# Other places for the sorted tokens, and other steps for the pairs, at the end of attention with routed experts on one core

## The chip, the core and the metric

The kernel runs on one core of a Trainium2 chip. A core has five engines that run beside each other, each with a queue of its own: TensorE (PE; its weight loads are PEld), VectorE (DVE), ScalarE (ACT), GpSimd (POOL) and SyncE (SP, which here issues most of the transfers). The metric is the device time of one execution in microseconds. A profile is a record of one execution; its span runs from the first to the last instruction of the program.

## What is computed

Four sequences of 1024 tokens with 512 features pass through attention with 16 heads of 32, then through a layer of 8 experts of rank 64 of which each token takes one; each half has a residual and a layer norm without weights.

```python
# x: (4, 1024, 512); wq, wk, wv, wo: (512, 512); A: (8, 64, 512); B: (8, 512, 64)
scores = einsum('bqhd,bkhd->bhqk', xq, xk)          # no scaling
probs  = softmax(scores)
x = layernorm(x + einsum('bhqk,bkhd->bqhd', probs, xv) @ wo.T)
p = softmax(x_flat @ Wr.T + br)
expert_idx, expert_weight = argmax(p), max(p)
h = einsum('nd,erd->ner', x_flat, A)
y = einsum('ner,eor->neo', h, B) / 64
x = layernorm(x + y[expert_idx] * expert_weight)
```

Everything is float32.

## The kernel before

**Attention.** A unit is one sequence and a group of four heads (GH = 4), 16 units in all; the last four, from LAST = 12 on, belong to the last sequence. Queries go in chunks of QC = 256 (NQ = 4 chunks), keys in tiles of 128 (NK = 8). `scores(s)` multiplies queries with keys (L290) and VectorE takes row maxima (L292); after every eighth step GpSimd splits the maxima into three bf16 parts (L192 to L197), which `turn_m` turns (L303). `weigh(s)` puts the maxima into four PSUM banks (L321), adds keys times queries (L330), and ScalarE takes exponentials into `probs` (L340). The sums of the exponentials, `dens`, are added by GpSimd (L344, L352) as long as maxima are still being taken 16 steps ahead, and by VectorE after that. `combine` multiplies with the values (L369) at every fourth step, and `settle` sums `dens` over keys (L388), takes the reciprocal on VectorE (L391) and scales (L393).

**After attention.** Class `After` treats one sequence. `project` multiplies with wo (L449) and adds the residual, `norm`, `choose` and `gate` make the first layer norm and the choice of the expert. `count` and `assign` give each token a place in a list sorted by experts, `scatter` (L561, an indirect DMA from GpSimd) writes tokens to `sorted_x` in device memory. Then the sorted tokens are treated in pairs of tiles of 128: `load_tokens` (L578, SyncE) reads pair k back, `turn_tokens` turns it (L607), `up` multiplies with A (L614), `down` with B (L623), VectorE adds (L626), `weigh_y` takes statistics (VectorE L409 to L411, GpSimd L402 to L404), `norm_y` scales (L414), and `store` writes two tiles to `out` with indirect DMAs from GpSimd (L641). The first three sequences have 8 pairs, the last has 7: its last 256 queries go through class `Last`, which multiplies with all experts at once (L726), masks (L734, L736), multiplies back (L741), adds (L745), and stores without sorting (L755).

**Tiles in rings.** A tile with a tag takes a place of a ring. Tag "h" has NT = 8 places of 128 x 514 and holds tokens of the sequences before sorting and, as `x`, after it; the last sequence's unsorted tokens lie elsewhere. So the two tiles of pair k take the places of pair k - 4, also across the border between two sequences, and their load waits for that pair's stores. Tag "k" has 5 places, one for the keys of each unit. Tag "probs" has 4.

**The order.** A loop runs over steps; step i weighs weights[i - 16] and takes scores of maxima[i], so that N = 272 is the first step after the last weighing. All else is a list of pieces. A `Piece` has a cost, a first and a last step, pieces that it comes after by a gap of steps, and things to be done so many steps later (`then`). A planner fills the steps in turn: it takes a piece that is due, or, while a step's cost is below a level worked out from what is left, one that is allowed. `r.step(k)` is the piece of a sequence's pairs: it holds `up` of pair k - 1, `down` of pair k - 2 and `turn_tokens` of pair k. Its `then` puts the statistics of pair k - 2 one step later, the norm GAP and the stores GAP + 1 steps later. `load_tokens(k)` stands one step ahead of piece k, the weights at pieces k and k + 1. At the end `keep_order` fixes this order on each engine, SyncE's too[...].

The steps of `r.step(k)` that the planner gives are, for the third sequence, 229, 234, 237, 240, 244, 250, 254, 261, 264, 268, and for the last, 265, 266, 269, 270, 272, 274, 275, 276, 278. The queries left to `Last` are projected in step 273, `up` is in 277, `mask` in 278, `down` in 279. The lines that set this are

```python
TAIL = [(N - 7, N - 6), (N - 6, N - 4), (N - 4, N - 3), (N - 3, N - 2)]
TAIL += [(N + i, N + i) for i in (0, 2, 3, 4, 6)]
...
            if b < B - 1:
                first, last_ = end + 17 + 3 * k, end + 25 + 4 * k
            else:
                first, last_ = TAIL[k]
```

where `end` is the step behind a sequence's last unit, 208 for the third.

Of the kernel before, what the change touches and what calls it, by code (L numbers as in the profile page):

```python
# [9 lines left out]
F32 = mybir.dt.float32  # L10
# [4 lines left out]
ALU = mybir.AluOpType  # L15
# [3 lines left out]
P = 128  # L19
HD = 32  # L20
GH = P // HD
QC = 256
# [19 lines left out]
def attention_then_experts(  # L42
# [18 lines left out]
    pe, act, dve, pool, sync = nc.tensor, nc.scalar, nc.vector, nc.gpsimd, nc.sync  # L61
    B, S, D = x.shape
    E = wr.shape[1]
    C = D // P
    NK = S // P
    NQ = S // QC
    TQ = QC // P
    NS = 2 * NK
    KP = NK // 2
# [4 lines left out]
    NT = S // P  # L74
    NX = 2 * NT
    W = D + 2
# [5 lines left out]
    work = ctx.enter_context(tc.tile_pool(name="work", bufs=2))  # L82
# [7 lines left out]
    def bank():  # L90
        turn_of[0] += 1
        return banks[(turn_of[0] - 1) % len(banks)]
# [32 lines left out]
    power = const.tile([P, TQ], F32, tag="power", name="power")  # L125
# [3 lines left out]
    for e in range(E):  # L129
# [5 lines left out]
        out=before_f,  # L135
# [33 lines left out]
    for t in spread_m:  # L169
# [5 lines left out]
        out=expand_f,  # L175
# [7 lines left out]
    expand = const.tile([E, E * R], BF16, tag="expand", name="expand")  # L183
# [25 lines left out]
    qT, kT, vS, mT, aT, top, probs, dens, both = ({} for _ in range(9))  # L209
# [51 lines left out]
    def project_k(u, x):  # L261

        if x.n == 0:
            kT[u] = work.tile([P, S], F32, tag="k", name="k", bufs=5)
        ps = bank()[:, :QC]
        for c in range(C):
            pe.matmul(ps, wk_sb[:, c, ts(units[u][1], P)], x.x[:, c, :], start=(c == 0), stop=(c == C - 1))  # L267
        act.copy(kT[u][:, ts(x.n, QC)], ps)
# [128 lines left out]

    def finish_stats(mv):

        rs = work.tile([P, 2, TQ], F32, tag="rs", name="rs", bufs=4)  # L400
        var = work.tile([P, TQ], F32, tag="var", name="var")
        pool.tensor_scalar_add(var, mv[:, :, 1], EPS)  # L402
        pool.tensor_tensor(rs[:, 0], var, power, ALU.pow)
        pool.tensor_tensor(rs[:, 1], mv[:, :, 0], rs[:, 0], ALU.mult)  # L404
        return rs

# [6 lines left out]
    def apply(h, rs, i):  # L413
        act.activation(h, h, AF.Identity, bias=rs[:, 1, i : i + 1], scale=rs[:, 0, i : i + 1])  # L414
# [42 lines left out]
    def stored(i):  # L457

        for other in stores:
            tc.declare_no_dep(i, other, reason="other rows")  # L460
        stores.append(i)

    class After:
# [110 lines left out]
        def load_tokens(self, k):  # L574
            assert len(self.scatters) == self.nt
            for i in range(2):
                self.x[k, i] = work.tile([P, W], F32, tag="h", name="x", bufs=NT)
                load = sync.dma_start(self.x[k, i], sorted_x[self.b][ts(2 * k + i, P), :]).ins  # L578
                for other in self.scatters:
                    tc.add_manual_dep(  # L580
                        load,
                        other.name,
                        mybir.DependencyInfo(mybir.DependencyClass.Sync, mybir.DependencyReason.DATA),
                        reason="any row",
                    )
# [81 lines left out]
    class Last:  # L667
# [58 lines left out]
                pe.matmul(ps, places["wu"][:, c, ts(k, P)], self.hT[:, c, :], start=(c == 0), stop=(c == C - 1))  # L726
            act.copy(self.u[:, k, :], ps)

        def mask(self):

            for k in range(0, C, 2):
                ps = bank()
                for i in range(2):
                    pe.matmul(ps[:, ts(i, QC)], expand[:, ts(k + i, P)], self.oT, start=True, stop=True)  # L734
                u = self.u[:, k : k + 2, :]
                dve.tensor_mul(u, ps.rearrange("p (i q) -> p i q", q=QC), u)  # L736

        def down(self, i, half):
            ps = bank()[:, :H2]
            for k in range(C):  # L740
                pe.matmul(  # L741
                    ps, self.u[:, k, ts(i, P)], places["wd"][:, k, ts(half, H2)], start=(k == 0), stop=(k == C - 1)
                )
            h = self.h[i][:, ts(half, H2)]
            dve.scalar_tensor_tensor(h, ps, self.gate[:, i : i + 1], h, ALU.mult, ALU.add)  # L745
            if half == 0:
                return
            if i == 0:
                self.mv = work.tile([P, TQ, 2], F32, tag="y_mv", name="y_mv2")
            self.add(self.mv, i)  # L750

        def finish(self):
            self.norm()
            for i in range(TQ):
                stored(sync.dma_start(out[B - 1, ts(TQ * self.n + i, P), :], self.h[i]).ins)  # L755

    N = len(weights) + NS
    COST_S, COST_T, COST_AV = 4 * 512, 512 + 4 * 512, 4 * NK * QC  # L760
    HALF = 4 * C * QC
# [27 lines left out]
    for i in range(len(weights)):  # L789
        base[i] += COST_S  # L790
        base[i + NS] += COST_T
        u, c, kp = weights[i]
# [18 lines left out]
    for u in range(1, LAST):  # L811
        for n in range(NQ):
            x_in = Load(units[u][0], n)
            first = max(start_of(u - 3) + KP * (n + 1), 0)
            for f in (project_q, project_k):
                Piece(lambda f=f, u=u, x_in=x_in: f(u, x_in), HALF, first, start_of(u - 1) - 1, load=x_in)
    for gs in ((0, 1), (2,), (3,)):
        for n in range(NQ):
            x_in = Load(B - 1, n)
            for g in gs:  # L820
                u = LAST + g
                first = max(start_of(LAST - 3) + KP * (g + 1), start_of(LAST - 4 + g))
# [3 lines left out]
    for n in range(1, NQ):  # L826
        for pair in ((0, 1), (2, 3)):
            x_in = Load(B - 1, n)
            first = start_of(LAST - 3 + n) + KP * (pair[1] + 1)
# [20 lines left out]
        return lambda i: i + k + (i + k in busy)  # L850


    TAIL = [(N - 7, N - 6), (N - 6, N - 4), (N - 4, N - 3), (N - 3, N - 2)]
    TAIL += [(N + i, N + i) for i in (0, 2, 3, 4, 6)]
    GAP = [2] * (B - 1) + [1]
    for b, r in enumerate(rest):
        end = start_of(C * b + C)
        for i in range(4):
            part = sorted_x[b].rearrange("(i j p) w -> i p j w", p=P, i=4)[i]
            early[min(start_of(b * C + i), start_of(LAST)) + 6 + (b == B - 1) * i].append(  # L860
                lambda part=part: sync.dma_start(part, nothing.unsqueeze(1).to_broadcast((P, NX // 4, W)))
            )
        p = None
        for t in range(r.nt):
            n, i = divmod(t, TQ)
            first = end - NS + KP * (n + 2)
            last_ = first + 5
            if b == B - 1:
                first = start_of(LAST) + NS * (n + 1) + KP
                last_ = first + 5  # L870
                if n == NQ - 2:
                    first = last_ = start_of(LAST) + NS * (n + 1) + 1 + i
            for half in range(2):
                then = []
                if i == TQ - 1 and half == 1:
                    if b < B - 1 or n < NQ - 2:
                        then = [(2, 0, r.norm, n), (step_without(2), 0, r.choose, n), (step_without(4), 0, r.gate, n)]
                    else:
                        then = [(1, 0, r.norm, n), (1, 0, r.choose, n), (2, 0, r.gate, n)]
                    if b < B - 1 and n == NQ - 1:  # L880
                        then += [(step_without(3), 600, r.count), (step_without(4), 0, r.assign)]
                        then += [(5 + k // 2, 0, r.scatter, k) for k in range(NT)]
                    elif b == B - 1 and n == NQ - 2:
                        then += [(2, 600, r.count), (3, 0, r.assign)]
                        then += [(3 + k // 3, 0, r.scatter, k) for k in range(r.nt)]
                p = Piece(
                    lambda r=r, t=t, half=half: r.project(t, half),
                    HALF,
                    first,
                    last_,  # L890
                    after=[(p, 0)] if p else (),
                    load=loads.setdefault((b, n), lambda r=r, n=n: r.load(n)),
                    then=then,
                )
        for k in range(r.nx // 2 + 2):
            if b < B - 1:
                first, last_ = end + 17 + 3 * k, end + 25 + 4 * k
            else:
                first, last_ = TAIL[k]
            p = Piece(  # L900
                lambda r=r, k=k: r.step(k),
                3 * 2200,
                first,
                last_,
                after=[(p, 3 if b < B - 1 else 1) if k else (p, 11 if b < B - 1 else 6)],
                then=[(-1, 0, r.weigh_y, k - 2), (GAP[b], 0, r.norm_y, k - 2), (GAP[b] + 1, 0, r.store, k - 2)]
                if k >= 2
                else [],
            )
            r.steps.append(p)  # L910
    last = {}

    def on_last(n, f, *args):
        def run():
            if n not in last:
                last[n] = Last(n)
            getattr(last[n], f)(*args)

        return run
# [15 lines left out]
                then=then,  # L935
            )
    for k in range(C):
        ups.append(Piece(on_last(n, "up", k), HALF, N + 5, N + 5, after=[(p, 4)]))
    q = Piece(on_last(n, "mask"), 1024, N + 6, N + 6, after=[(o, 1) for o in ups])
    for i in range(TQ):  # L940
        for half in range(2):
            done = i == TQ - 1 and half == 1
            then = [(1, 0, on_last(n, "finish"))] if done else []
            Piece(on_last(n, "down", i, half), HALF, N + 7, N + 7, after=[(q, 1)], then=then)

# [141 lines left out]
```

## Time and profile before

| | us |
|---|---|
| three runs | 1526.82, 1527.3, 1531.33 (median 1527.3) |
| the profiled execution | 1522.7 |
| its span | 1520.9 |
| TensorE busy | 1451.4 (95%) |
| GpSimd busy | 1186.0 (78%) |
| VectorE busy | 992.9 (65%) |
| ScalarE busy | 749.7 (49%) |
| GpSimd's additions L352 and L344 | 837.7 and 141.4 |
| TensorE's mean granted clock | 0.983 of full speed |

Busy shares are means over stages with different limits[...]. So the page is read for where the digits of a row change along the span, and then stretch by stretch: busy time of each engine in a stretch, what each engine waited for, and the chain of waits, which follows the last instruction back to what released it. In a row of the timeline stand start, duration, engine (with a q for its queue), line, operation, tiles written and read, shapes, count, and in brackets the engine's idle time before it and what ended that.

### The profile page before, as it was taken

To read this page: it belongs to the slowest core of one execution; us is meant where nothing else is said; L and a number is where in the kernel's file an instruction comes from. 1 tells how busy PE (TensorE), PEld (TensorE's weight loads), DVE (VectorE), ACT (ScalarE), POOL (GpSimd) and SP (SyncE) were. 2 spreads that over 40 slices of the span, in tenths; PEclk is the share of its full clock that TensorE was granted. 3 is DMA by queue.
4 is the path that set the end of the run, shared out by engine and by line. 5 is a ranking of instruction groups with operands and counts; after the bars stand their busy time and mean duration, and the time that the engine had idled before them with its cause. 6 is when DMAs were issued, how large, how long until landed. Compare 5 with 4: busy or idle time off the path is not lost.

```text
span 1520.9 us, 37286 instructions
## 1 busy us (share of the span) xinstructions
PE 1451.4 (95%) x15100; PEld 933.0 (61%) x15100; DVE 992.9 (65%) x1853; ACT 749.7 (49%) x1527; POOL 1186.0 (78%) x949
## 2 busy tenths in 40 slices
PE   7999999999999999999999999999999999999675
PEld 6666666666666666666666666666666565555344
DVE  1546666666776576676677557776877668776743
ACT  1125555554445555555444546555445556565532
POOL 2019999998778899899878988999998999972333
PEclk9999999999999999999999999999999999999877
DMA  7422212122102524332110523433411402221241
GB/s 236 139 83 72 71 43 71 43 85 84 57 16 84 167 82 142 107 104 71 33 52 30 181 65 118 153 99 103 139 67 57 149 19 67 81 66 57 77 146 42
DMA packets 101051, 135.25 MB, mean 89 GB/s; under 512 B 9077, under 2 KB 71301, under 8 KB 100880
## 3 DMA queue, kind: packets, MB, share of 16 engines
q1 hardware_dynamic: 91072, 113.92, 23.8%
q0 software_dynamic: 7696, 16.85, 3.1%
q8 instruction: 119, 1.95, 0.5%
q10 hardware_dynamic: 2112, 2.10, 0.4%
q14 instruction: 52, 0.43, 0.1%
HBM read 99.70 MB, written 41.52 MB: 93 GB/s over the span
## 4 chain that ended last, share of the span: by engine, by line
PE 79%; POOL 7%; ACT 4%; DVE 4%; issue 3%; DMA 2%; POOLq 0%; SPq 0%; ACTq 0%; DVEq 0%
PE bank L369 13%; PE bank L290 12%; PE bank L330 12%; PE bank L276 8%; PE bank L257 8%; PE bank L267 7%; PE bank L449 7%; POOL dens L352 5%; PE bank L321 5%; ACT probs L340 3%; PE bank L388 2%; PE bank L623 2%; PE bank L607 1%; PE bank L614 1%; DVE top L292 1%
## 5 line engine op out<-in xcount | busy, mean ns | idle before, releaser
L352 POOL TENSOR_TENSOR dens<-dens,probs 128x1024 f32<-128x1024 f32 x355 | 837.7, 2360 | 92.7 <-ACT probs L340 71.8
L292 DVE TENSOR_REDUCE top<-bank 128x1 f32<-128x512 f32 x1024 | 635.9, 683 | 416.2 <-PE bank L290 416.0
L340 ACT ACTIVATE probs<-bank 128x512 f32<-128x512 f32 x1024 | 528.3, 602 | 278.1 <-PE bank L330 262.0
L290 PE MATMUL bank<-k,q 32*128 32x512 f32 x2048 | 287.1, 594 | 1.2 <-DVE slot_i L541 0.8
L330 PE MATMUL bank<-q,k 32*128 32x256 f32 x4096 | 268.6, 376 | 0.0
L369 PE MATMUL bank<-probs,v 128*32 128x256 f32 x4096 | 237.0, 381 | 1.8 <-ACT probs L340 1.7
L330 PEld LDWEIGHTS bank<-q,k 32*128 32x128 f32 x4096 | 202.7, 185 | 18.3 <-issue 2.6
L369 PEld LDWEIGHTS bank<-probs,v 128*32 128x32 f32 x4096 | 129.4, 110 | 100.2 <-ACT probs L340 20.4
L344 POOL TENSOR_TENSOR dens<-probs 128x1024 f32<-128x1024 f32 x60 | 141.4, 2356 | 8.8 <-ACT probs L340 8.5
L257 PE MATMUL bank<-xT,wq 128*128 128x256 f32 x512 | 128.5, 395 | 8.7 <-DMA xT<-in_xt 7.9
L449 PE MATMUL bank<-wo,aT 128*128 128x264 f32 (+1 forms) x512 | 122.2, 389 | 6.0 <-ACT probs L340 4.3
L257 PEld LDWEIGHTS bank<-xT,wq 128*128 128x128 f32 x512 | 93.6, 192 | 55.9 <-ACT probs L340 33.2
L290 PEld LDWEIGHTS bank<-k,q 32*128 32x128 f32 x2048 | 110.9, 184 | 26.5 <-issue 5.4
L267 PE MATMUL bank<-xT,wk 128*128 128x256 f32 x512 | 123.7, 386 | 3.2 <-ACT probs L340 3.1
L276 PE MATMUL bank<-wv,xT 128*128 128x256 f32 (+1 forms) x512 | 124.3, 390 | 1.2 <-ACT probs L340 0.7
L391 DVE RECIPROCAL bank<-bank 128x256 f32<-128x256 f32 x64 | 112.5, 1758 | 18.6 <-PE bank L388 18.6
L449 PEld LDWEIGHTS bank<-wo,aT 128*128 128x128 f32 x512 | 94.4, 190 | 41.6 <-ACT probs L340 26.6
L267 PEld LDWEIGHTS bank<-xT,wk 128*128 128x128 f32 x512 | 94.9, 190 | 38.3 <-ACT probs L340 26.3
L276 PEld LDWEIGHTS bank<-wv,xT 128*128 128x128 f32 x512 | 93.9, 190 | 34.6 <-ACT probs L340 17.5
L321 PE MATMUL bank<-mT,ones_b 3*128 3x512 bf16 x1024 | 108.5, 387 | 3.6 <-ACT probs L340 1.7
L377 ACT COPY both<-bank 128x256 f32<-128x256 f32 x64 | 23.8, 373 | 176.7 <-PE bank L369 176.7
L641 POOL DMA_INDIRECT out<-x x62 | 63.3, 1021 | 33.0 <-issue 15.3
(132 smaller groups left out, 974.0 us busy)
## 6 DMA issues: line engine op xcount, KB each, us to landing
xT<-in_xt SPq DMA_DIRECT2D x98, 512.0 KB, 3.6
sorted<-nothing SPq DMA_DIRECT2D x16, 1028.0 KB, 7.0
x<-sorted SPq DMA_DIRECT2D x62, 257.0 KB, 3.0
wa<-in_wa SPq DMA_DIRECT2D x62, 128.0 KB, 2.2
wb<-in_wb SPq DMA_DIRECT2D x62, 128.0 KB, 3.2
h<-in_x SPq DMA_DIRECT2D x28, 256.0 KB, 3.8
wo<-in_wo POOLq DMA_DIRECT2D x1, 1024.0 KB, 6.2
wv<-in_wv ACTq DMA_DIRECT2D x2, 512.0 KB, 13.1
```

The source lines that it names most:

```text
L257: pe.matmul(ps, wq_sb[:, c, ts(units[u][1], P)], x.x[:, c, :], start=(c == 0), stop=(c == C - 1))
L267: pe.matmul(ps, wk_sb[:, c, ts(units[u][1], P)], x.x[:, c, :], start=(c == 0), stop=(c == C - 1))
L276: pe.matmul(ps, x.x[:, c, ts(t, P)], wv_sb[:, c, columns(h)], start=(c == 0), stop=(c == C - 1))
L290: pe.matmul(ps, q[r, ts(t % TQ, P)], kT[u][r, ts(n, 512)], start=True, stop=True)
L292: dve.tensor_reduce(top[i][:, here // 2, j, n : n + 1], ps, axis=AX.X, op=ALU.max, negate=True)
L321: pe.matmul(ps.rearrange("p (k q) -> p k q", q=QC), ones_b[r, :], m[r, :].unsqueeze(1).to_broadcast((NP, 2, QC)), start=True, stop=False,)
L330: pe.matmul(ps[:, ts(k, QC)], kT[u][r, ts(2 * kp + k, P)], qT[u, c][r, :], start=False, stop=(k == 1),)
L340: act.activation(pr[:, :, j, :], ps.rearrange("p (k q) -> p k q", q=QC), AF.Exp)
L344: adder.tensor_add(dens[u, c], pr[:, 0].rearrange("p j q -> p (j q)"), pr[:, 1].rearrange("p j q -> p (j q)"),)
L352: adder.tensor_add(dens[u, c], dens[u, c], pr[:, k].rearrange("p j q -> p (j q)"))
L369: pe.matmul(ps[j * HD : (j + 1) * HD, :], v[:, k, col : col + HD], probs[u, c, k // 2][:, k % 2, j, :], start=(k == 0), stop=(k == NK - 1),)
L449: pe.matmul(ps, aT[b, c, n][:, ts(i, P)], wo_sb[:, c, columns(half)], start=(c == 0), stop=(c == C - 1))
```

## The change

The sorted tokens of the last sequence's pairs 0 to 4 lie in the ring "k", one place for both tiles of a pair, and the places of this ring become 128 x 1028 instead of 128 x 1024. Pairs 5 and 6 stay in "h".

```diff
-            kT[u] = work.tile([P, S], F32, tag="k", name="k", bufs=5)
+            kT[u] = work.tile([P, max(S, TQ * W)], F32, tag="k", name="k", bufs=5)
...
-                self.x[k, i] = work.tile([P, W], F32, tag="h", name="x", bufs=NT)
+                if self.b < B - 1 or k >= 5:
+                    self.x[k, i] = work.tile([P, W], F32, tag="h", name="x", bufs=NT)
+                elif i == 0:
+
+                    pair = work.tile([P, max(S, TQ * W)], F32, tag="k", name="x_pair", bufs=5)
+                    self.x[k, 0], self.x[k, 1] = (pair[:, ts(j, W)] for j in range(TQ))
```

The third sequence's pieces get steps of their own (SPREAD, counted from step 208), and the last sequence's get later ones (TAIL). The pieces of `project` of the first three sequences are bound to two steps.

```diff
-    TAIL = [(N - 7, N - 6), (N - 6, N - 4), (N - 4, N - 3), (N - 3, N - 2)]
-    TAIL += [(N + i, N + i) for i in (0, 2, 3, 4, 6)]
+    SPREAD = [18, 21, 24, 28, 30, 33, 36, 40, 42, 45]
+    TAIL = [(N - 4, N - 4), (N - 3, N - 3), (N - 2, N - 2)] + [(N + i, N + i) for i in (0, 2, 3, 4, 5, 7)]
...
-            first = end - NS + KP * (n + 2)
-            last_ = first + 5
+            first = end - NS + KP * (n + 2) + 1
+            last_ = first + 1
...
-            if b < B - 1:
+            if b < B - 2:
                 first, last_ = end + 17 + 3 * k, end + 25 + 4 * k
+            elif b == B - 2:
+                first = last_ = end + SPREAD[k]
             else:
                 first, last_ = TAIL[k]
...
-                after=[(p, 3 if b < B - 1 else 1) if k else (p, 11 if b < B - 1 else 6)],
+                after=[(p, 3 if b < B - 2 else 1) if k else (p, 11 if b < B - 1 else 9)],
```

The planner then gives 226, 229, 232, 236, 238, 241, 244, 248, 250, 253 for the third sequence and 268, 269, 270, 272, 274, 275, 276, 277, 279 for the last.

In `Last`, `up` and `mask` go by halves (two blocks of `up` in step 277 and two in 278, the masks one step behind each), `down` is in step 280, and each row of tokens has statistics by halves, a norm and a store of its own; `finish` is gone, and `finish_stats` takes one column or two.

```diff
     for k in range(C):
-        ups.append(Piece(on_last(n, "up", k), HALF, N + 5, N + 5, after=[(p, 4)]))
-    q = Piece(on_last(n, "mask"), 1024, N + 6, N + 6, after=[(o, 1) for o in ups])
+        ups.append(Piece(on_last(n, "up", k), HALF, N + 5 + k // 2, N + 5 + k // 2, after=[(p, 4)]))
+        if k % 2:
+            q = Piece(on_last(n, "mask", k - 1), 512, N + 6 + k // 2, N + 6 + k // 2, after=[(ups[-1], 1)])
...
             if half == 0:
+                self.st = work.tile([P, 2, 6], F32, tag="st2", name="st2")
+            dve.bn_stats(self.st[:, half, :], h)
+            if half == 0:
                 return
-            if i == 0:
-                self.mv = work.tile([P, TQ, 2], F32, tag="y_mv", name="y_mv2")
-            self.add(self.mv, i)
-
-        def finish(self):
-            self.norm()
-            for i in range(TQ):
-                stored(sync.dma_start(out[B - 1, ts(TQ * self.n + i, P), :], self.h[i]).ins)
+            mv = work.tile([P, 1, 2], F32, tag="y_mv2", name="y_mv2")
+            dve.bn_aggr(mv[:, 0, :], self.st)
+            dve.tensor_scalar_mul(mv[:, 0, 0:1], mv[:, 0, 0:1], -1.0)
+            apply(self.h[i], finish_stats(mv), 0)
+            stored(sync.dma_start(out[B - 1, ts(TQ * self.n + i, P), :], self.h[i]).ins)
```

More of the change, by code (lines that the diff above doesn't have):

```diff
@@ L398, in finish_stats @@
     def finish_stats(mv):
-        rs = work.tile([P, 2, TQ], F32, tag="rs", name="rs", bufs=4)
-        var = work.tile([P, TQ], F32, tag="var", name="var")
+        n = mv.shape[1]
+        rs = work.tile([P, 2, TQ], F32, tag="rs", name="rs", bufs=4)[:, :, :n]
+        var = work.tile([P, TQ], F32, tag="var", name="var")[:, :n]
         pool.tensor_scalar_add(var, mv[:, :, 1], EPS)
-        pool.tensor_tensor(rs[:, 0], var, power, ALU.pow)
+        pool.tensor_tensor(rs[:, 0], var, power[:, :n], ALU.pow)
         pool.tensor_tensor(rs[:, 1], mv[:, :, 0], rs[:, 0], ALU.mult)
@@ L727, in up, with mask @@
             act.copy(self.u[:, k, :], ps)
[L729 to L736, printed above, removed]
+        def mask(self, k):
+            ps = bank()
+            for i in range(2):
+                pe.matmul(ps[:, ts(i, QC)], expand[:, ts(k + i, P)], self.oT, start=True, stop=True)
+            u = self.u[:, k : k + 2, :]
+            dve.tensor_mul(u, ps.rearrange("p (i q) -> p i q", q=QC), u)
         def down(self, i, half):
@@ L937, in attention_then_experts @@
     for k in range(C):
-        ups.append(Piece(on_last(n, "up", k), HALF, N + 5, N + 5, after=[(p, 4)]))
-    q = Piece(on_last(n, "mask"), 1024, N + 6, N + 6, after=[(o, 1) for o in ups])
+        ups.append(Piece(on_last(n, "up", k), HALF, N + 5 + k // 2, N + 5 + k // 2, after=[(p, 4)]))
+        if k % 2:
+            q = Piece(on_last(n, "mask", k - 1), 512, N + 6 + k // 2, N + 6 + k // 2, after=[(ups[-1], 1)])
     for i in range(TQ):
         for half in range(2):
-            done = i == TQ - 1 and half == 1
-            then = [(1, 0, on_last(n, "finish"))] if done else []
-            Piece(on_last(n, "down", i, half), HALF, N + 7, N + 7, after=[(q, 1)], then=then)
+            Piece(on_last(n, "down", i, half), HALF, N + 8, N + 8, after=[(q, 1)])
     for i in range(len(base)):
```

## The prediction

> **What bounds the kernel now.** I counted steps first. A step of the loop weighs once, so it leaves four L321 matmuls on TensorE; every fourth group of them in the timeline begins a step, from step 16 (100.9 us) to step 271 (1453.2 us). In which step each piece stands comes from the instruction order of the two built programs. Then I read the page, busy time by stretch, the chain of waits, and the timeline of the stretch that the chain led to.
>
> ```profile
> PE   7999999999999999999999999999999999999675
> ...
> POOL 2019999998778899899878988999998999972333
> ...
> PE 79%; POOL 7%; ACT 4%; DVE 4%; issue 3%; DMA 2%; POOLq 0%; SPq 0%; ACTq 0%; DVEq 0%
> ```
>
> TensorE carries the chain, but not to the end: its last slices fall to 6 and 7, and GpSimd is full before. Busy time of the engines by stretch, in the order TensorE, its weight loads, VectorE, ScalarE, GpSimd, then clock:
>
> ```profile
> 1047.00:1183.00 136.00, 134.16 (x1384) 86.37 (x1377) 100.58 (x221) 68.13 (x136) 125.28 (x100) 1.00 0.30 98
> 1184.00:1344.00 160.00, 153.85 (x1763) 92.73 (x1759) 117.08 (x213) 87.93 (x175) 149.44 (x113) 1.00 0.25 77
> ...
> 1437.00:1450.00 13.00, 2.00 (x6) 0.43 (x5) 5.76 (x12) 1.67 (x3) 8.27 (x10) 0.50 0.14 34
> 1450.00:1458.00 8.00, 6.61 (x56) 3.75 (x58) 0.00 (x0) 3.24 (x6) 0.00 (x0) 0.51 0.96 284
> ```
>
> Three regimes. Steps 196 to 220 (1047 to 1183) are TensorE's: 134 of 136 us. Steps 221 to 254 (1184 to 1361) are GpSimd's: 149 of 160 us, the rest mostly the pauses at its DMA issues, and the chain there runs from one denominator addition (L352) to the next. From step 256 on VectorE does these additions, so GpSimd is free, and there is a hole of 12.6 us:
>
> ```profile
> 1447.03 1.66 SPq L578 DMA_DIRECT2D x<-sorted  x2
> ...
> 1449.68 0.71 PEld L607 LDWEIGHTS bank<-ident,x 128*128 128x128 f32 x4 [12.57 <-DMA x<-sorted]
> ...
> 1455.45 4.78 PE L369 MATMUL bank<-probs,v 128*32 128x256 f32 x64
> ```
>
> Pair 3 of the last sequence is to be turned (L607) in step 270, but its tokens lie in the ring "h" of eight tiles, in the slots of the third sequence's pair 7, which is only being stored then. The queue's own waits from 1360 us on name it: L578 on the stores, 41.1 us in 9 waits.
>
> **The change, part by part**, against the profiled execution (span 1520.9 us, 1522.7 us in all).
>
> *(a) Project pieces two to a step, one step later, for sequences 0 to 2.* For 0 and 1 the same pieces trade places within steps 72 to 165; both programs carry the same work, and TensorE is full there: 0 (between -2 and +2). For the third sequence, pinning its 16 pieces makes the planner pull other projections ahead: steps 196 to 220 hold four pieces more. One is "L257 x8" of 1.93 us, nothing is idle to take it: **+7.7 us** at step 221 (bounds +4 and +8). Steps 221 to 228 lose them again, where GpSimd, not TensorE, sets the pace.
>
> *(b) The third sequence's pairs in steps 226 to 253* (before 229 to 268). TensorE's work of steps 221 to 255 is the same within 0.2% of the planner's units, since the pieces pulled ahead make room. GpSimd's is not. Up to its last addition it now holds 8 groups of pair statistics instead of 4, and 14 stores instead of 8. The rows:
>
> ```profile
> 1285.74 1.08 POOL L641 DMA_INDIRECT out<-x  x1 [0.17 <-issue]
> 1287.12 1.00 POOL L641 DMA_INDIRECT out<-x  x1 [0.30 <-issue]
> 1288.14 0.25 POOL L402 TENSOR_SCALAR var<-y_mv 128x2 f32<-128x2 f32 x1
> 1288.47 0.72 POOL L403 TENSOR_TENSOR rs<-var,power 128x2 f32<-128x2 f32 x1
> 1289.28 0.20 POOL L404 TENSOR_TENSOR rs<-y_mv,rs 128x2 f32<-128x2 f32 x1
> ...
> 1344.08 2.35 POOL L344 TENSOR_TENSOR dens<-probs 128x1024 f32<-128x1024 f32 x1 [2.40 <-ACT probs L340]
> 1348.79 2.35 POOL L352 TENSOR_TENSOR dens<-dens,probs 128x1024 f32<-128x1024 f32 x1 [2.36 <-ACT probs L340]
> ```
>
> A pair's stores take 0.17 + 1.08 + 0.30 + 1.00 = 2.55 us, a group of statistics 1.3 us: 3 x 2.55 + 4 x 1.3 = 12.9 us more on the engine that sets the pace. It idled 2.40 + 2.36 us at the end, which it will not when late: **+8.1 us**. Bounds 0 (all of it slack) and +12.9. The settling in step 256 waits for the last addition, which ends at 1361.2 us, within a us of TensorE: no cover is left.
>
> *(c) The ring "h" gets tighter for the third sequence.* Pair k+4 waits for the stores of pair k, issued three steps after piece k+2; piece k+4 follows piece k+2 by 6, 5, 6 and 7 steps where it followed by 7 to 11. GpSimd ends a step's additions 8 to 14 us after TensorE began the step, then 2.6 us of issue, 2.7 us to landing, 3.0 us of load: pair 4's tokens come some 20 us after step 235 began, pair 5's 22 us after step 239 began. At the mean step of 5.06 us the turning in steps 238 and 241 is reached after some 17 and 13 us, so TensorE would stand 3 and 9 us. Behind the waiting L578, SyncE's queue holds the weights wa and wb of the same pairs, wanted a step later or more. GpSimd meanwhile has 10 to 12 us of additions queued and hardly starves: bounds 0 and 12, I take **+2 us**. The scatter into "sorted" must also have landed three steps sooner (step 225), but there step 226 waits for GpSimd's L197 as it does now.
>
> Here a rule speaks against the change. Row: behind the hole the clock is 0.51 for 8 us, and the combination took 4.78 us against 3.5 us elsewhere. "TensorE: Matmul & The Clock Gate" (What's actually happening) says that an idle window of some 3.4 us halves the clock, and about as much work restores it. By the rule the 9 us stand makes 3.4 us of work cost 1.7 us more; by the row, 8 us of work cost 4. I charge nothing in the sum, for GpSimd is the bound there, and the row's 4 us to a rival.
>
> *(d) The last sequence's pairs in the slots of the keys, pieces from step 268 on.* Pairs 0 to 4 take slots of heads' keys last read in steps 207, 259, 263, 267 and 271, their loads stand in steps 267, 268, 269, 271 and 273: no wait. The hole and the half clock behind it go. Late next are VectorE and the exponentials.
> - Step 261 to 264, 18.5 us before. The third sequence's turning goes, but weighing 262 and 263 still need banks that VectorE holds for counting (to 1389.8 us) and assigning (1393.1 us). Then 1.2 of weighing and 3.5 of combination, so 264 begins near 1397.8 instead of 1401.2: -3.4.
> - 264 to 268, 20.0 us before: three pieces go. Left are 4 weighings of 1.3, a combination of 3.5, a settling of 1.5, and about 2.5 until VectorE's reciprocal frees a bank: 12.7, so -7.3.
> - 268 to 271, 32.0 us before with the hole. Left: 3 weighings 3.9, a settling 1.5, one turning 1.1, up and turning 2.2, a whole piece 3.3, and 0.5: 12.5, so -19.5.
> - 271 to the last projections: 11.3 us before at half clock in part, 10.3 after: -1.0. Then one pair piece more than before (pieces k = 4 to 8 instead of 5 to 8), +3.3.
>
> Sum **-27.9 us**. It is bounded by the hole and half clock alone, -12.6 - 4 = -16.6, and by -32.
>
> *(e) The last two rows of queries.* Up and mask in halves: TensorE no longer waits 1.5 us for VectorE before L741: -1.5. Statistics by halves and a row at a time: the last bn_stats covers 256 elements, half of 0.69 us: -0.3. GpSimd has one group of 1.3 us more, the first row's, which lies beside the second row's matmuls. The last two indirect stores still come behind the last statistics, so the end is not otherwise shorter: **-1.8**. Bounds 0 and -3.
>
> Sum: 7.7 + 8.1 + 2 - 27.9 - 1.8 = **-11.9 us**. On the profiled execution that is 1510.8 us; the median shown, 1527.3, lies 4.6 above the profiled one, so I forecast **1515.4 us**.
>
> **Rivals.**
> 1. *The store-bound ring (slower).* In steps 226 to 253 the pairs follow the stores so closely that TensorE stands 1.5 + 3 + 9 + 3 us at L607, starves GpSimd each time, and restarts at half clock (+4). In place of 2: 20.5, so 1533.9. For it: nine waits of L578 on stores already. Against: GpSimd has two steps of additions in hand. It decides once GpSimd itself idles for ScalarE in steps 238 to 250 for over 12 us.
> 2. *Only the hole goes.* Step 261 to 271 is bound by VectorE's additions and ScalarE (2.06 us a step) as much as by TensorE, so moving pieces out frees just 16.6 us: 1527.3 + 17.8 - 16.6 - 1.8 = 1526.7, no change. For it: VectorE was busy 11.9 of the 16 us from 1421 on. Against: part of that was the moved pieces' own.
> 3. *GpSimd's stretch absorbs its new work*, with bounds 4, 0 and 0: 4 - 29.7 = 1501.6. Against: 149 of 160 us.
> 4. *The change does not do what it says*: keys end late and x_pair waits for them. The key reads above exclude it, up to 2%.
>
> **Numbers.** Forecast 0.58 (own range 1507 to 1523), ring 0.16, only the hole 0.14, absorbed 0.10, other 0.02. What this measurement can tell from no change is 0.3%, 4.6 us. Faster: most of the forecast, absorbed and a share of the third, 0.69; same 0.15; slower 0.16. The range, 1502 to 1530, takes in the absorbed case, the forecast, the hole case, and half of what the ring can cost.
>
> **What will show it.** Right: no L607 waits above 3 us after 1400, TensorE's clock 1.00 near the end of weighing, ten steps from 261 to 271 in about 40 us instead of 70; step 221 some 8 us late and the last L352 on GpSimd some 16 us late. Wrong: L607 waiting for "x<-sorted" in steps 226 to 250 with GpSimd idle, or a new wait between steps 262 and 268 on VectorE.

## The result, and the profile after

The changed kernel takes 1522.92 us (median of 11 runs, 1520.71 to 1524.58), the kernel before 1527.49 us (11 runs, 1526.54 to 1531.33). The ratio is 0.9963, with a 95% interval of 0.9954 to 0.9973: 0.37% faster, 5.6 us by the ratio and 4.6 us between the medians, where 11.9 us had been forecast. The profiled execution took 1521.64 us, its span 1519.9.

The rows of the page of the changed kernel that answer to those shown before, TensorE and GpSimd in 40 slices, and the shares of the chain:

```profile
PE   7999999999999999999999999999999999899785
...
POOL 2019999997778999899878989999877999884124
...
PE 85%; DVE 5%; ACT 4%; issue 3%; DMA 1%; POOL 1%; POOLq 0%; ACTq 0%; SPq 0%; DVEq 0%
```

GpSimd has almost left the chain (7% to 1%), and the dip to 6 in TensorE's row is gone. The time did not follow. Busy time by stretch of the changed kernel (columns as in the prediction):

```profile
1286.00:1305.00 19.00, 12.04 (x134) 7.41 (x128) 11.58 (x21) 6.74 (x14) 17.34 (x17) 0.87 0.21 65
...
1374.00:1390.00 16.00, 15.60 (x156) 7.84 (x158) 7.23 (x16) 5.75 (x12) 12.08 (x17) 0.79 0.01 1
...
1409.00:1426.00 17.00, 11.22 (x128) 6.83 (x131) 11.31 (x24) 7.43 (x15) 7.14 (x6) 0.70 0.22 82
...
1441.00:1453.00 12.00, 11.13 (x148) 7.54 (x144) 6.76 (x6) 9.28 (x20) 0.00 (x0) 1.00 0.27 74
```

The last row holds steps 268 to 270, where the hole was: TensorE is busy in 11.1 of 12 us at full clock. The other three rows are losses at lower clocks.

Counting the fours of L321 again gives where each step begins. The first column is the first profile of the kernel before, in us; the others are differences to it, of a second profile of the same kernel, of the changed kernel, and of four experiments that follow.

| step | before | again | changed | spare_ring | spare_fewer_stores | old_spread | both_old |
|---|---|---|---|---|---|---|---|
| 196 | 1047.5 | +2.2 | +1.2 | +1.2 | +1.4 | -1.0 | +2.7 |
| 221 | 1183.4 | +2.9 | +8.5 | +8.5 | +8.7 | +8.5 | +2.7 |
| 240 | 1278.1 | +2.9 | +10.2 | +10.3 | +10.5 | +6.6 | +7.0 |
| 242 | 1285.7 | +2.9 | +19.1 | +11.6 | +11.8 | +6.2 | +7.0 |
| 244 | 1297.0 | +2.9 | +18.6 | +10.9 | +10.6 | +7.5 | +7.0 |
| 245 | 1302.1 | +2.9 | +19.0 | +15.7 | +11.0 | +7.5 | +7.0 |
| 255 | 1354.9 | +2.9 | +19.4 | +15.8 | +11.6 | +7.3 | +7.0 |
| 256 | 1360.6 | +3.1 | +26.1 | +22.5 | +18.0 | +7.5 | +7.0 |
| 264 | 1401.2 | +4.9 | +25.1 | +21.8 | +18.3 | +9.3 | +8.7 |
| 268 | 1421.2 | +4.9 | +19.5 | +16.1 | +11.5 | +6.7 | +6.1 |
| 271 | 1453.2 | +4.6 | -0.3 | -3.7 | -8.4 | -8.9 | -7.9 |
| span | 1520.9 | +4.6 | -1.0 | -4.3 | -9.5 | -9.2 | -8.5 |

The changed kernel enters step 256 by 26.1 us later and gives all of it back by step 271; the forecast had 17.8 us for the one and 30.2 for the other. Of the 17.6 us that it loses from step 221 on, 8.9 arise in steps 240 and 241 and 6.7 in step 255. The first profile of the kernel before lies below the median of its runs; the second, 4.6 us longer, lies at it, and against it the changed span is 5.6 us shorter, as the runs say. The profiled execution of both_old is the slowest of its five, 8.1 us above their median, so its column stands too high.

### The profile page after: what moved, and what is told of

It is laid out like the page before. It is cut to its first block, busy times and chain, and to the rows that moved or that the text cites. A ratio compares the mean times of both kernels' runs of the same rounds, so it can differ in the third digit from the quotient of the medians.

```text
span 1519.9 us, 37296 instructions
## 1 busy us (share of the span) xinstructions
PE 1455.6 (96%) x15100; PEld 937.8 (62%) x15100; DVE 993.0 (65%) x1855; ACT 749.4 (49%) x1527; POOL 1179.7 (78%) x952
## 4 chain that ended last, share of the span: by engine, by line
PE 85%; DVE 5%; ACT 4%; issue 3%; DMA 1%; POOL 1%; POOLq 0%; ACTq 0%; SPq 0%; DVEq 0%
PE bank L369 14%; PE bank L290 13%; PE bank L330 13%; PE bank L276 8%; PE bank L257 8%; PE bank L450 7%; PE bank L267 7%; PE bank L321 5%; ACT probs L340 3%; PE bank L388 2%; PE bank L629 2%; PE bank L613 2%; PE bank L620 2%; DVE top L292 1%; DMA xT<-in_xt 1%
## 5 line engine op out<-in xcount | busy, mean ns | idle before, releaser
L340 ACT ACTIVATE probs<-bank 128x512 f32<-128x512 f32 x1024 | 528.3, 603 | 298.9 <-PE bank L330 279.6
L290 PE MATMUL bank<-k,q 32*128 32x512 f32 x2048 | 295.9, 596 | 1.9 <-DVE slot_i L542 1.0
L330 PE MATMUL bank<-q,k 32*128 32x256 f32 x4096 | 273.5, 380 | 0.0
L330 PEld LDWEIGHTS bank<-q,k 32*128 32x128 f32 x4096 | 206.6, 187 | 22.5 <-issue 7.0
L369 PEld LDWEIGHTS bank<-probs,v 128*32 128x32 f32 x4096 | 129.6, 111 | 100.2 <-ACT probs L340 16.3
L344 POOL TENSOR_TENSOR dens<-probs 128x1024 f32<-128x1024 f32 x60 | 141.4, 2356 | 7.5 <-ACT probs L340 7.0
L290 PEld LDWEIGHTS bank<-k,q 32*128 32x128 f32 x2048 | 115.1, 185 | 31.6 <-issue 5.7
L321 PE MATMUL bank<-mT,ones_b 3*128 3x512 bf16 x1024 | 113.6, 388 | 11.6 <-DVE aT L393 5.7
L276 PEld LDWEIGHTS bank<-wv,xT 128*128 128x128 f32 x512 | 93.5, 190 | 36.9 <-ACT probs L340 19.8
L450 PEld LDWEIGHTS bank<-wo,aT 128*128 128x128 f32 x512 | 94.7, 190 | 32.3 <-ACT probs L340 16.6
L321 PEld LDWEIGHTS <-ones_b 3*128 3x128 bf16 x1024 | 28.7, 91 | 101.5 <-issue 100.9
```

The lines of the kernel that those rows point to most:

```text
L276: pe.matmul(ps, x.x[:, c, ts(t, P)], wv_sb[:, c, columns(h)], start=(c == 0), stop=(c == C - 1))
L290: pe.matmul(ps, q[r, ts(t % TQ, P)], kT[u][r, ts(n, 512)], start=True, stop=True)
L321: pe.matmul(ps.rearrange("p (k q) -> p k q", q=QC), ones_b[r, :], m[r, :].unsqueeze(1).to_broadcast((NP, 2, QC)), start=True, stop=False,)
L330: pe.matmul(ps[:, ts(k, QC)], kT[u][r, ts(2 * kp + k, P)], qT[u, c][r, :], start=False, stop=(k == 1),)
L340: act.activation(pr[:, :, j, :], ps.rearrange("p (k q) -> p k q", q=QC), AF.Exp)
L344: adder.tensor_add(dens[u, c], pr[:, 0].rearrange("p j q -> p (j q)"), pr[:, 1].rearrange("p j q -> p (j q)"),)
```

## The experiments

Each is a kernel of its own, timed against the kernel before on the same chip, so ratios are compared, not microseconds. One per mille is 1.5 us.

**places_alone.** Only the diff of `project_k` and `load_tokens`, on the kernel before; every step as before.

> The kernel before with one part of the change: the last sequence's pairs 0 to 4 in the ring of the keys, all steps as before. Theory A (the hole ahead of step 271 is the ring's alone, and the moved steps then cost more than they bring): the hole of 12.6 us and the half clock behind it go, nothing else moves, 1527.5 - 16.6 = about 1511 us, faster than the whole change (1522.9). Theory B (VectorE's additions bound steps 261 to 271 anyway, the pieces must leave there too): most of the hole comes back as waits for VectorE, about 1520 us or more.

Measured: ratio 0.9926 (0.991 to 0.9943), so 11.3 us less, twice what the whole change brings. Step 256 to 271 takes 80.6 us instead of 92.6. Theory A holds in kind, with 11 to 12 us instead of 16.6: behind the removed hole TensorE still waits twice for ScalarE, 2.5 us in step 270 and 2.4 us in step 271. So the rest of the change loses 5 us or more in sum.

**old_project.** The whole change with the project pieces in their old windows.

```diff
-            first = end - NS + KP * (n + 2) + 1
-            last_ = first + 1
+            first = end - NS + KP * (n + 2)
+            last_ = first + 5
```

> The whole change with the project pieces of sequences 0 to 2 in their old windows of six steps; the pairs' steps stay as in the change. Theory A (the 8.5 us by which step 221 is late come from pinning these pieces, and nothing behind gives them back): step 221 about 2 us late instead of 8.5, the time about 1517 us. Theory B (steps 221 to 255 are paced by GpSimd or the ring, which absorb an earlier start): step 221 early, but step 256 as late as now, about 26 us, and the time stays near 1522.

Measured: ratio 0.9936 (0.992 to 0.9953), 4.1 us better than the whole change. From step 180 to 221 the lateness grows by 2.8 us, with the whole change by 9.1. Theory A: the pinning costs, and nothing behind it absorbs an earlier start.

**spare_ring.** The third sequence's pairs 4 and 5 in the place that wd takes later.

```diff
+                if self.b == B - 2 and k in (4, 5):
+                    if "spare" not in places:
+                        places["spare"] = work.tile([P, NK * (H2 + E)], F32, tag="v", name="x_spare", bufs=3)
+                    self.x[k, i] = places["spare"][:, ts(2 * (k - 4) + i, W)]
...
-    early[start_of(LAST) + 10].append(lambda: take("wd", work, "v", 3, D, wb.rearrange("e r d -> (e r) d")))
+    def take_wd():
+        places["wd"] = places["spare"][:, : C * D].rearrange("p (c d) -> p c d", d=D)
+        sync.dma_start(places["wd"], wb.rearrange("e r d -> (e r) d").rearrange("(c p) o -> p c o", p=P))
+
+    early[N - 10].append(take_wd)
```

> The whole change with the third sequence's pairs 4 and 5 in a place of the values' ring that the last weights take later (their load moves to step 262), so that no pair of that sequence waits for stores of a pair close ahead; steps as in the change. Theory A (the ring's stand in step 241 put 10 us on the path): no wait of L613 for tokens in steps 238 and 241, step 256 some 16 us late instead of 26, the time about 1513 us. Theory B (GpSimd's 12.9 us of added work pace this stretch, and the stand lay beside it): the wait goes, but step 256 is still late by 22 us or more, and the time stays above 1519.

In the whole change the stand is there, in step 241. From its chain of waits, the pieces in order of time (start, duration, what):

```profile
1292.81 2.36 POOL dens L352
1296.44 0.52 issue
1297.20 2.80 DMA out<-x
1300.05 2.62 DMA x<-sorted
1302.81 2.04 PE bank L613 x8
```

Addition, store of pair 1, its landing, the load of pair 5, its turning: one behind the other, as the prediction had drawn it. TensorE's timeline of the whole change:

```profile
1302.81 2.04 PE L613 MATMUL bank<-ident,x 128*128 128x128 f32 x8 [6.60 <-DMA x<-sorted]
...
1305.18 1.90 PE L330 MATMUL bank<-q,k 32*128 32x256 f32 x16
```

TensorE waited 6.60 us for the tokens, and at the clock that followed the next L330 group took 1.90 us instead of 1.03. Measured without it: ratio 0.9929 (0.9912 to 0.9945), 5.2 us better. But the table shows that only half of the early gain stays: 7.5 us at step 242, 3.3 at 245. TensorE runs ahead until GpSimd's lateness reaches it in step 244 (the next experiment shows how). Neither theory alone is right; step 256 is 22.5 us late, which is theory B's number, and the time lies between.

**spare_fewer_stores.** As spare_ring, and three pairs are not stored; that part of the output is left out.

```diff
         def store(self, k):
+            if self.b == B - 2 and k < 3:
+                return
```

> As spare_ring, but the third sequence's pairs 0 to 2 are not stored (six indirect DMAs left out, their rows of the output stay unwritten), all else in its place. GpSimd loses 3 x 2.55 = 7.7 us of work ahead of step 243. Theory A (GpSimd sets the pace from the scatter to step 243): the addition of step 243 ends 6 to 8 us earlier than in spare_ring, step 256 earlier by 4 us or more, the time by as much. Theory B (TensorE and VectorE set it there too): no change beyond 1.5 us.

Measured: ratio 0.9898 (0.988 to 0.9916), 4.7 us better than spare_ring, though the two intervals overlap a little. GpSimd's timeline of spare_ring first, then of this kernel; the rows are the same group of statistics and the three additions of steps 242 and 243.

```profile
1307.16 0.99 POOL L651 DMA_INDIRECT out<-x  x1 [0.15 <-issue]
1308.46 0.98 POOL L651 DMA_INDIRECT out<-x  x1 [0.30 <-issue]
...
1309.69 0.25 POOL L403 TENSOR_SCALAR var<-y_mv 128x2 f32<-128x2 f32 x1
...
1310.98 7.21 POOL L352 TENSOR_TENSOR dens<-dens,probs 128x1024 f32<-128x1024 f32 x3
```

```profile
1301.69 0.22 POOL L403 TENSOR_SCALAR var<-y_mv 128x2 f32<-128x2 f32 x1
...
1302.95 7.26 POOL L352 TENSOR_TENSOR dens<-dens,probs 128x1024 f32<-128x1024 f32 x3
1311.57 2.36 POOL L344 TENSOR_TENSOR dens<-probs 128x1024 f32<-128x1024 f32 x1 [1.35 <-ACT probs L340]
```

1310.98 against 1302.95: the additions come 8.0 us earlier for 7.7 us of stores taken away. So GpSimd's queue does cost time here (theory A), but not step by step: both kernels begin step 244 at the same time, 1307.9 and 1307.6 us, and in that one step spare_ring loses 4.4 us against the other. The timeline of spare_ring shows the way:

```profile
1311.06 1.52 ACT L415 ACTIVATE x<-x,rs 128x512 f32<-128x512 f32 x2 [2.22 <-POOL rs L405]
...
1313.11 1.30 PE L624 MATMUL bank<-xsT,wa 128*64 128x128 f32 x16 [3.10 <-ACT probs L340]
```

ScalarE's norm waits for GpSimd's statistics, the exponentials (L340) stand behind that norm, TensorE waits 3.10 us for them, and the granted clock is at half for 3.4 us from 1313.9 us on. Without the stores GpSimd is not the late one: in spare_fewer_stores it idles 1.35 us at L344, waiting for ScalarE, and step 256 gains only 4.5 of the 8.0 us.

**old_spread.** The whole change with the third sequence's pairs in their old windows.

```diff
-            if b < B - 2:
+            if b < B - 1:
                 first, last_ = end + 17 + 3 * k, end + 25 + 4 * k
-            elif b == B - 2:
-                first = last_ = end + SPREAD[k]
...
-                after=[(p, 3 if b < B - 2 else 1) if k else (p, 11 if b < B - 1 else 9)],
+                after=[(p, 3 if b < B - 1 else 1) if k else (p, 11 if b < B - 1 else 9)],
```

> The whole change with the third sequence's pairs in windows as before instead of the pinned steps; the planner then gives 226, 233, 236, 240, 244, 250, 254, 261, 265, 269. Theory A (pulling three pieces ahead of step 256 costs what it saves behind, plus the ring's stand): step 256 about 10 us late instead of 26, steps 256 to 271 some 8 us longer again, a net gain of about 6 us, 1517. Theory B (VectorE and the count bound the stretch behind 256 so that a piece there costs its full 5 us and more): the time goes up, 1525 or more.

Measured: ratio 0.9906 (0.9886 to 0.9926), 8.7 us better than the whole change. Step 256 begins 18.6 us sooner; steps 256 to 271 take 76.2 us against 66.2, so 10.0 us come back. Theory A, with both sizes larger than written.

**pool_later and stats_later.** The whole change; of the third sequence's pairs 4 to 7, first GpSimd's part and then VectorE's part too stand in steps 257 to 261.

```diff
+            late = (lambda i, k=k: N - 21 + k) if b == B - 2 and k >= 6 else None
...
-                then=[(-1, 0, r.weigh_y, k - 2), (GAP[b], 0, r.norm_y, k - 2), (GAP[b] + 1, 0, r.store, k - 2)]
+                then=[
+                    (-1, 0, r.weigh_y, k - 2),
+                    (GAP[b] if late is None else late, 0, r.norm_y, k - 2),
+                    (GAP[b] + 1 if late is None else lambda i, k=k: N - 20 + k, 0, r.store, k - 2),
+                ]
```

In pool_later `norm_y` of these pairs calls `finish_stats` itself, and the tile with the means and variances gets five places; in stats_later `weigh_y` is whole, and its gap is `-1 if late is None else late` too.

> The whole change, but for the third sequence's pairs 4 to 7 GpSimd's part of the statistics, the norm and the stores stand in steps 257 to 261 instead of 245 to 256; VectorE's part and TensorE's pieces stay. GpSimd loses some 13 us of work ahead of step 256. Theory A (GpSimd sets the pace only up to step 243; behind it TensorE and VectorE do): step 256 as late as with the whole change, within 2 us, the time 1521 to 1524. Theory B (GpSimd sets the pace up to step 254, as the prediction had it): step 256 earlier by 8 us or more, the time about 1515.

> As pool_later, and VectorE's part of the statistics of pairs 4 to 7 in steps 257 to 260 too. Theory A (VectorE's queue is what holds TensorE in steps 253 to 255: the reductions of row maxima stand behind a reciprocal, an addition and these statistics, and the wait drops the clock to half in the combination of step 255): that combination takes 3.5 us instead of 5.96, step 256 earlier by 4 to 7 us, the time about 1517 to 1519. Theory B (VectorE's statistics lie beside TensorE's work): as pool_later, and the moved statistics make steps 257 to 260 longer.

Measured: pool_later 0.9991 (0.9983 to 1.0), stats_later 1.0023 (1.0016 to 1.0029), both slower than the whole change. From step 221 to 256 pool_later loses 17.7 us, the whole change 17.6: GpSimd does not set the pace late in that stretch, theory A of the first. Its numbers for the time fail, though, since the moved work stands ahead of the last choice of experts: step 260 is 4.9 us longer, with a wait of TensorE for that choice (L435) of 4.84 us. For stats_later the place is shown. VectorE's queue and TensorE in steps 253 to 255 of the whole change (timeline):

```profile
1370.23 1.75 DVE L391 RECIPROCAL bank<-bank 128x256 f32<-128x256 f32 x1
...
1372.88 1.40 DVE L632 SCALAR_TENSOR_TENSOR x<-bank,x 128x512 f32<-128x512 f32 x2
...
1374.20 0.68 DVE L410 BATCH_NORM_STATS2 st<-x 128x6 f32<-128x512 f32 x1
...
1376.21 4.28 DVE L292 TENSOR_REDUCE top<-bank 128x1 f32<-128x512 f32 x7
...
1376.94 3.86 PE L290 MATMUL bank<-k,q 32*128 32x512 f32 x8 [0.40 <-DVE top L292]
...
1380.74 5.96 PE L369 MATMUL bank<-probs,v 128*32 128x256 f32 x64
```

Seven reductions stand behind the reciprocal, the addition of the pair and its statistics, the scores L290 creep after them from bank to bank, and then the combination takes 5.96 us. In pool_later, which has VectorE's statistics in the same place, and in stats_later, which has not:

```profile
1378.47 5.35 PE L369 MATMUL bank<-probs,v 128*32 128x256 f32 x64
```

```profile
1375.12 3.66 PE L369 MATMUL bank<-probs,v 128*32 128x256 f32 x64
```

Steps 254 and 255 are 5.0 us shorter in stats_later than in the whole change, and 3.6 us shorter than in pool_later, from which it differs by VectorE's statistics alone. From step 245 to 256 the six profiles that have the pinned pairs' statistics in place lose 5.2 to 7.1 us against the first profile of the kernel before; stats_later loses 0.7, and the five kernels with these pairs in their old windows lose at most 0.3. That much of theory A is right; what it did not see is the price of the same work in steps 257 to 260: step 259 became 8 us longer, and 263 nearly 3.

**last_alone.** The kernel before with the diff of `Last` (and of `finish_stats`) alone.

> The kernel before with only the last part of the change: up and mask of the last 256 queries by halves, statistics by halves, each row normed and stored by itself, down one step later. Theory A (as predicted): 1.8 us less, ratio 0.9988. Theory B (the last indirect stores end the program whatever the rows do, and the mask's wait is only moved): no change, ratio 1.000.

Measured: ratio 0.9965 (0.995 to 0.9979), 5.3 us less, three times theory A. GpSimd's last rows before, then in last_alone:

```profile
1507.98 0.22 POOL L402 TENSOR_SCALAR var<-y_mv 128x2 f32<-128x2 f32 x1 [6.59 <-DVE y_mv L410]
...
1509.89 1.05 POOL L641 DMA_INDIRECT out<-x  x1 [0.63 <-issue]
1511.24 0.99 POOL L641 DMA_INDIRECT out<-x  x1 [0.30 <-issue]
```

```profile
1498.37 1.05 POOL L642 DMA_INDIRECT out<-x  x1 [1.14 <-ACT x L415]
1499.72 0.98 POOL L642 DMA_INDIRECT out<-x  x1 [0.30 <-issue]
...
1503.55 0.23 POOL L403 TENSOR_SCALAR var<-y_mv 128x1 f32<-128x1 f32 x1 [1.64 <-DVE y_mv L752]
```

With `down` one step later and the pairs' last piece still in 278, the last indirect stores stand ahead of the last statistics, and the end is the last row's own short chain. In the whole change that piece went to step 279, and the stores are last again (1508.92 and 1510.30 us, of a span of 1519.9).

**whole_early_end, both_old, both_old_early_end.** The whole change, and the whole change with both undoings; "early_end" is

```diff
-    TAIL = [(N - 4, N - 4), (N - 3, N - 3), (N - 2, N - 2)] + [(N + i, N + i) for i in (0, 2, 3, 4, 5, 7)]
+    TAIL = [(N - 4, N - 4), (N - 3, N - 3), (N - 2, N - 2)] + [(N + i, N + i) for i in (0, 2, 3, 4, 5, 6)]
```

> The whole change with both the project pieces and the third sequence's pairs in windows as before; what stays is the keys' ring, the later steps of the last sequence's pairs, and the last rows by halves. Theory A (the two losses add: 5 us of pinned project pieces, 9 us of pinned pairs): the gains of the two single undoings add up, 1522.9 - 4.1 - 9.3 = about 1509 us, ratio 0.988. Theory B (they overlap, since the stretch of steps 221 to 255 takes up an earlier start): no better than old_spread, 1513 to 1515.

> The whole change with nothing but that last piece in step 278 instead of 279. Theory A: the last indirect stores start ahead of the last rows' statistics, the span ends 2 to 4 us sooner, ratio to before about 0.994. Theory B: 0.996, as the whole change.

> As both_old, and the last pair's last piece in step 278 as before instead of 279, so that its two indirect stores stand in step 280 ahead of the last rows' statistics on GpSimd's queue. Theory A (in last_alone the gain of 5 us came from these stores leaving the end): 2 to 4 us less than both_old, ratio to before about 0.985 to 0.986. Theory B (it came from the halves and rows alone): as both_old, 0.988.

Measured: both_old 0.988 (0.986 to 0.9901): the two losses add, theory A; that the digits agree is luck, with an interval of 0.2% to either side. whole_early_end 0.9945 (0.9928 to 0.9961), 2.7 us better than the whole change, and both_old_early_end 0.9859 (0.984 to 0.9877), 3.2 us better than both_old. The intervals of each pair overlap, so the runs alone do not settle these two; the profiles do, for both: from step 271 to the end 63.2 us instead of 67.0, and 63.7 instead of 67.1, where the eight profiles with the piece in step 279 have 66.6 to 67.5. both_old_early_end is the fastest kernel of the study, 1.4% (21.5 us) below the kernel before.

**before_again.** No edit.

> The kernel before once more, for a second profile: the first profiled execution was 4.8 us below the median of its other runs. If the spread lies in one place, a stretch of the early steps should be longer here by 3 to 5 us with all later stretches alike; if it lies everywhere, the steps drift apart slowly.

Measured: 1527.3 us, span 1525.5. The two profiles run alike but for a few steps that differ by 0.6 to 1.8 us, in steps 96, 160 and 263 above all. It lies neither in one place nor everywhere.

## Why the prediction was wrong, step by step

The direction held, the size did not: 5.6 us by the ratio, 4.6 between the medians, where 11.9 stood. The step that failed is in part (b). It prices the three pairs that move ahead of step 256 as work of GpSimd alone, and of the rest it says only that TensorE's work "is the same within 0.2% of the planner's units, since the pieces pulled ahead make room". VectorE's part of these pairs, 3.4 us each in the timeline of the changed kernel (the addition and the statistics), is in no term of the sum. Up to step 245 the sum came out: 10.5 us from step 221 on, where (b) and (c) make 10.1. From step 245 to 256 it has nothing, and there the changed kernel loses 7.1 us, the last 6.7 in step 255, behind VectorE's queue and at a lower clock; with VectorE's statistics moved away 0.7 us are left (stats_later).

TensorE's work was in sum as stated. By the planner's units the changed kernel has 9784 less in steps 221 to 229 and 9104 more in steps 230 to 255, 4.6 and 4.3 us at the 2130 units a us of steps 196 to 220. The room brought next to nothing: from step 221 to 230 the changed kernel gains 0.1 us, and its chain of waits leaves TensorE there, for ScalarE's exponentials and, from 1209.8 to 1218.3 us, for GpSimd.

- *(a), +7.7.* Steps 196 to 220 are 7.3 us longer with their four pieces more, about as priced; steps 180 to 195 are 1.8 us longer, and the planner has one piece more in steps 166 to 195, which was not counted. Ahead of that, where nothing was charged, the pinning seems to gain: from step 16 to 180 the seven profiles with pinned pieces take 0.5 to 3.4 us less than the first profile of the kernel before, the seven without them 0 to 2.7 us more. So the undoing gives 6.3 us in the profiles from step 180 to 221, but 4.1 by the runs. Right in mechanism, too high by 3.6.
- *(b), GpSimd +8.1.* As a size it was good. The three additions of step 243, in the kernel before and in the changed one:

```profile
1294.43 7.24 POOL L352 TENSOR_TENSOR dens<-dens,probs 128x1024 f32<-128x1024 f32 x3
```

```profile
1310.73 7.24 POOL L352 TENSOR_TENSOR dens<-dens,probs 128x1024 f32<-128x1024 f32 x3
1319.54 2.35 POOL L344 TENSOR_TENSOR dens<-probs 128x1024 f32<-128x1024 f32 x1 [1.57 <-ACT probs L340]
```

They come 16.3 us later, of which 8.5 were there at step 221, so 7.8; without the ring's stand (spare_ring) 7.1 us are on TensorE's path at step 245. But that GpSimd bounds the stretch up to step 254 was wrong: behind these additions it waits for ScalarE, and its last one ends at 1384.1 us, 2.6 us before step 256 begins; in the kernel before it ended 0.6 us after step 256 had begun.
- *(c), the ring, +2.* The stand came in step 241, 6.6 us of waiting where 9 had been drawn, and none in step 238 for the 3 drawn there; its cost on the path is 3.6 us at step 256 and 5.2 by the runs. Undersized. It overlaps with (b): the two together are the 10.5 us, and with the stand gone 7.1 of them stay. Of the two prices for the clock, that of the Trainium skill ("TensorE: Matmul & The Clock Gate", What's actually happening) was nearer: the clock was at half from 1300 to 1307 us by the records, of which the last 4 us were work, so some 2 us were lost, where the rule made 1.7 and the row 4. The reason given for taking 2, that GpSimd has additions in hand, holds: 4 of the 7.5 us gained at step 242 were lost again to GpSimd by step 245.
- *(d), -27.9.* Step 256 to 271 gained 26.4 us of the 30.2 that its parts make up to there; behind step 271 0.7 us more came, where (d) and (e) have 0.5 the other way. By parts: 261 to 264 gained 1.4 of 3.4, 264 to 268 gained 5.6 of 7.3, 268 to 271 gained 19.8 of 19.5. The two short ones are waits for VectorE's reciprocal and the count, which were named, and a half clock that came with them, which was not charged: 10.2 us from 1412.8 us on and 3.4 us from 1433.2 on. In the timeline of the changed kernel:

```profile
1413.68 0.58 PE L321 MATMUL bank<-mT,ones_b 3*128 3x512 bf16 x1 [2.99 <-DVE aT L393]
...
1416.39 0.61 PE L321 MATMUL bank<-mT,ones_b 3*128 3x512 bf16 x2 [2.13 <-DVE slot_i L542]
...
1433.23 0.58 PE L321 MATMUL bank<-mT,ones_b 3*128 3x512 bf16 x1 [2.76 <-DVE aT L393]
1433.23 2.28 PE L330 MATMUL bank<-q,k 32*128 32x256 f32 x16
```

The group of the last row takes 1.03 us at full clock. A new wait for VectorE between steps 262 and 268 was named as a sign of being wrong, and it came.
- *(e), -1.8.* That the last stores stay last was right for this change. The 1.8 us by themselves were not measured. What it would bring to have the stores first was not asked; it is 3 us.

Of the rivals, the store-bound ring was real, at a quarter of its price. "Only the hole goes" falls: it gave steps 261 to 271 a gain of 16.6 us, and they gained 26.8. "GpSimd's stretch absorbs its new work" falls with spare_fewer_stores, though its 4 us for (a) came true.

With the measured sizes in the places of the terms, (a) by the runs and the others by the profiles, the sum is 4.1 + 10.5 + 7.1 - 26.4 - 0.7 = -5.4 us. It was in part luck that it fell no shorter: (a) had been charged 3.6 us too much. The undoings close too: 21.5 us for the best form, less 3 for the last stores, less 8.7 for the pinned pairs, less 4.1 for the pinned projections, leaves 5.7, and 5.6 were measured. What the later steps of the last sequence's pairs bring by themselves was not tried; the best form has 4.9 us more than places_alone and last_alone together, about what the intervals of the three leave open, so that no gain of theirs is shown.

## What to carry to other kernels

Work that moves must be priced on every engine that takes part in it, at the steps where it lands. Here the part of GpSimd, the fullest engine beside TensorE, came out within 0.4 us together with the ring, and the part of VectorE, busy for 65% of the span and left out for that stretch, cost 7 us in a few steps. When a wait for a buffer is the defect, try the buffer alone first; here the places were worth 11 us, and the schedule that came with them gave half of it back. And look at what stands last on every queue at the end of the program: one step's difference in the order of two small stores was 3 us.

## What was not expected

Executions of one kernel differ by a few steps of 0.6 to 1.8 us, some of them in places that repeat (step 263 is longer by 1.7 to 1.8 us in four of these profiles), so a single profile can lie 4.8 us from the median, that of both_old even 8.1; with an effect of that size, two profiles of the kernel before are needed to read one difference.
